# Block 0's first ff product by 26 products, the side work of five stages in another order, and the last quarter of shift and scale loaded by halves

## The chip, the cores and the metric

The kernel runs on one core of one Trainium2 chip. The time is the device time of one execution in microseconds (us), as the median of several runs. The engines of the core take their instructions in order, each from its own queue: PE (TensorE, matrix products), DVE (VectorE), ACT (ScalarE), POOL (GpSimd) and SP (SyncE, which here only issues transfers). PE's row of records has two for each matmul of a 128x256 tile.

## The reference

Two sequences of 2048 tokens with 512 features, and one condition vector of 512 for each sequence:

```
emb = silu(t) @ ada_w + ada_b
shift_msa, scale_msa, gate_msa, shift_mlp, scale_mlp, gate_mlp = split(emb, 6)
norm  = ln(x) * (1 + scale_msa) + shift_msa
h     = gelu(norm @ ssm_w1 + ssm_b1, exact)
x     = x + gate_msa * (h @ ssm_w2 + ssm_b2)
norm2 = ln(x) * (1 + scale_mlp) + shift_mlp
hf    = gelu(norm2 @ ff_w1 + ff_b1, tanh)
x     = x + gate_mlp * (hf @ ff_w2 + ff_b2)
```

All is float32. ssm_w1 and ssm_w2 are 512x512, ff_w1 is 512x1024 and ff_w2 1024x512.

## The kernel before

**Blocks and stages.** The 4096 tokens are worked in eight blocks of 512, four to a sequence, and a block stays in SBUF from its load to its store. Each has four stages: hA (first ssm product with its gelu), oA (second ssm product and residual), hC (first ff product with its gelu), oC (second ff product and residual). The stages of different blocks are interleaved; the first ones run in the order hA_0, oA_0, hA_1, oA_1, hC_0, hA_2, oC_0, hC_1. A block's norm is named n1_i ahead of hA_i and n2_i ahead of hC_i.

**Products.** No stage multiplies its matrices plainly. `group` (L573) splits both operands in four and makes seven products in place of eight, with places named P1 to P7; their order in a stage is P1, P2, P6, P5, P7, P3, P4, or, in the first three stages, P1, P2, P5, P6, P7, P3, P4. Some operands of the seven are sums of quarters: sums of weights are made once, sums of tokens (`summed`) for each block. hC of block 0 is two such groups of four matmuls a product, so 56 matmuls. From block 1 on, hC is `Second.products` (L1280) instead: a table `HK_P` of 26 products of two matmuls each, whose operands are 28 registers of weights and 24 of tokens; a row of the table names the bank of PSUM, whether it starts afresh, the two registers, and the eight parts of the result that read the bank behind it, with their signs. The tables `HK_A` (37 sums on the weights, in place) and `HK_B` (20 sums on the tokens) say how the registers come from the operands; `sums_of_registers` (L1221) issues them, each 128x256.

A part of the result is first written by ACT from PSUM, later reads are added by DVE (L1324 and L1327), and its bias and gelu follow on ACT (L1305). The next product into the same bank waits for the reads of the last.

```
for n, (b, fresh, ra, rb, reads) in enumerate(HK_P):
    for j in range(2):
        nc.tensor.matmul(ps[b][:, j, :], fa[ra][...], fb[rb]...., start=(fresh and j == 0), ...)
```

**Side work.** All that isn't a matmul of a stage is hung as small functions on the places of the stage (`hook`), and is issued right behind the product of that place, to whichever engine it uses. No scheduler moves anything: the order of the code is the order on each engine, so an instruction that waits holds up all behind it on its engine. For a norm the side work is: statistics (`mixed_stats` puts three of the four pieces on ACT, as sums and squares, and one on DVE), `root` (`ve` on DVE, a power `r` on POOL, L682 and L683) and `rest` (a Newton step on DVE), `normal` (ACT), `turn` (a transpose in 32x32 squares on DVE, L757), `move` (16 transfers of 64 KB that place the squares, on SP's and ACT's queues, L766), `moved` (shift and scale, L794), and the token sums. Further side work: the rows of the adaLN product (`rows_of`, 16 or 32 narrow matmuls on PE, L287), their transposition and bias (`modulation`), gates, the folding of gates into second weights, the residual's seeds, and loads.

**Head.** Shift and scale of the ssm branch come from the first 1024 columns of ada_w, loaded by rows of the matrix in three transfers of 1 MB, 0.5 MB and 0.5 MB (`load_ada_01`) on SP's queue, ahead of w1 in two halves. `rows_01` multiplies, `modulation_01` turns the result and adds the bias, and the tokens of block 0, transposed by PE (L773), are modulated by quarters of the features and halves of the tokens on ACT (L794) and DVE (L796). P1 of hA_0 reads features 0 to 255, P2 features 256 to 511.

**Around the change.** Weight sums of fw1: block 0's seven products need four sums of 128x1024 on POOL (`fw1_sums`, in oA_0 to oA_1). The 37 sums of `HK_A` for the later blocks follow on DVE from hC_0's second group to the end of oC_0, behind a reload of a quarter of fw1 that the earlier sums have overwritten. fw2's folds run on DVE in oA_1 and hC_0, its sums on POOL.

Of the kernel before, what the change touches and what calls it, by code (L numbers as in the profile page):

```python
# [45 lines left out]
    (1, '-', 1, 0),  # L46
    (3, '+', 3, 1),
    (11, 'n', 10, 11),
    (27, '+', 11, 1),
    (26, '-', 27, 8),  # L50
    (25, '+', 13, 15),
    (25, '-', 25, 12),
    (24, '-', 27, 2),
    (23, '-', 3, 24),
    (8, '+', 8, 23),
    (8, '+', 0, 8),
    (22, '-', 12, 26),
    (21, 'n', 1, 22),
    (22, '+', 2, 22),
    (9, '-', 9, 11),  # L60
    (20, '-', 6, 27),
    (10, '+', 6, 10),
    (19, '-', 9, 10),
    (19, 'n', 26, 19),
    (0, '-', 4, 0),
    (23, '-', 23, 0),
    (4, '+', 4, 27),
    (27, '-', 6, 19),
    (2, '-', 27, 2),
# [39 lines left out]
    (5, True, 26, 20, ((5, -1), (7, 1))),  # L109
# [3 lines left out]
    (5, False, 8, 21, ((1, 1),)),  # L113
# [6 lines left out]
    (5, False, 23, 12, ((3, 1),)),  # L120
    (0, False, 24, 16, ((0, 1),)),
    (1, True, 11, 8, ((0, -1), (2, -1))),
    (5, False, 4, 10, ((2, 1),)),
    (0, False, 2, 23, ((4, -1), (5, -1))),
    (3, False, 27, 1, ((3, 1),)),
    (5, False, 0, 9, ((0, 1),)),
# [9 lines left out]

HK_BANK = {5: "y", 2: "x", 4: "v", 0: "x", 1: "y", 3: "v"}
# [3 lines left out]
def kernel(  # L141
# [22 lines left out]
    C = 4  # L164
# [133 lines left out]
    def rows_01(pa, ks):  # L298

        for k in ks:  # L300
            w = ada_01[k // 2][:, k % 2].rearrange("p (g n m q) -> p g m n q", g=2, n=KD, q=G)
            for g in range(2):
                for m in range(P // G):
                    nc.tensor.matmul(
                        pa[m * G : (m + 1) * G, g * P : (g + 1) * P],
                        silu[:, k, :],
                        w[:, g, m],
                        start=(k == 0 and g == 0),
                        stop=(k == KD - 1),
                        tile_position=(0, m * G),  # L310
                        skip_group_check=True,
                    )

    def modulation_01(pa):

        turned = pa[:, 2 * P : 4 * P]
        nc.vector.transpose(turned, pa[:, : 2 * P])
        turned = turned.rearrange("p (g n q) -> p g n q", g=2, n=KD)
        m = const.tile([P, 2, KD, B], F32, tag="mod_0", name="mod_0")
        bias = colsT[:, R_ADA : R_ADA + 2 * KD].rearrange("p (g n) -> p g n", g=2)  # L320
        nc.vector.tensor_tensor(m, turned[:, :, :, :B], bias.unsqueeze(3).to_broadcast([P, 2, KD, B]), ALU.add)
        for part in range(2):
            mods[0, part] = m[:, part]
# [253 lines left out]
    def group(name, kdim, lhs, rhs, after, hooks, parted=(), order=ORDER, places=None):  # L577
# [4 lines left out]
        for p, place in zip(order, places or order):  # L582
# [7 lines left out]
            for j in range(2):  # L590
                for k in range(kdim):
# [24 lines left out]
    class Norm:  # L616
# [17 lines left out]
        def mixed_stats(self):  # L634

            sums, var = self.sums_on_act(), self.squares_on_act(D**-0.5)
            return sums[:3] + var[:4], self.stats(self.mv)[3:]

        def sums_on_act(self):
# [3 lines left out]
            self.unread = work.tile([P, C, D], F32, tag="blocks", name=f"unread{n}")  # L643
# [109 lines left out]
        def turn(self, c):  # L753
# [6 lines left out]
            )  # L760

# [460 lines left out]
    def sums_of_registers(program, reg, engs, copied=None, beside=()):  # L1222


        def op(n, d, f, a, b):
# [4 lines left out]
            elif f == "n":  # L1230
                nc.vector.scalar_tensor_tensor(reg[d], reg[a], -1.0, reg[b], ALU.mult, ALU.subtract)
# [38 lines left out]
    class Second:  # L1270
# [9 lines left out]
        def products(self, fa, fb, hooks, act_first=False):  # L1280


            ends = {b: n for n, (b, *_) in enumerate(HK_P)}
            starts = [(n, b) for n, (b, fresh, *_) in enumerate(HK_P) if fresh]
            stops = set(ends.values())
            for n, b in starts:
                stops |= {max([m for m in range(n) if HK_P[m][0] == b], default=ends[b])}
# [678 lines left out]
```

## Time and profile before

| | us |
|---|---|
| median of 3 runs | 577.23 (577.11 to 578.51) |
| profiled execution | 577.13 |
| its span | 575.3 |
| around the span | 1.83 |
| hC_0, seven products, 56 matmuls | 24.36 |
| hC_1, 26 products, 52 matmuls | 22.45 |

In the chain of work that ended last a row is a start, a length, an engine, the tile written and the line: `68.22 1.73 PE py_hC L592 x8` is one product of hC_0, eight records of PE. In the timeline `out<-in` names the tiles; what stands in brackets at a row's end is the engine's idle time ahead of it and what ended it. The clock granted to PE was 1.00 in every stage shown.

### The profile page before, as it was taken

The numbers are of one execution on the slowest core, as the hardware profiler recorded it, in microseconds if no ns is written. First come the engines' busy times: TensorE is split into PE (matmuls) and PEld (weight loads), VectorE is DVE, ScalarE is ACT, GpSimd is POOL, SyncE is SP. The second block draws the span as 40 slices with busy tenths as digits, with TensorE's granted clock in tenths as the row PEclk, the third lists the DMA queues.
The fourth block names the chain that finished last, engine by engine and source line by source line (L and its number), as shares of the span: only waits on it lengthen the run. The fifth ranks groups of instructions, "written<-read, shape, count | busy, mean of one in ns | idle before, by whom it ended". The sixth has DMA issues, their size and how long they took to land.

```text
span 575.3 us, 10190 instructions
## 1 busy us (share of the span) xinstructions
PE 570.6 (99%) x3467; PEld 514.5 (89%) x3467; DVE 451.9 (79%) x984; ACT 296.5 (52%) x585; POOL 439.2 (76%) x460
## 2 busy tenths in 40 slices
PE   9999999999999999999999999999999999999997
PEld 4888888888899889998899988998889999899897
DVE  4968898897789376977869877996768598897676
ACT  3727457706834875448734588325655431732430
POOL 1665449999997869889898999998994885378361
PEclk9999999999999999999999999999999999999999
DMA  8977433304205503283042921243240240031002
GB/s 329 388 232 250 101 71 92 96 38 146 63 13 148 219 2 70 96 260 126 1 93 56 338 100 24 52 108 122 101 110 1 110 131 18 1 75 74 1 1 73
DMA packets 26863, 62.30 MB, mean 108 GB/s; under 512 B 5136, under 2 KB 6204, under 8 KB 25148
## 3 DMA queue, kind: packets, MB, share of 16 engines
q1 hardware_dynamic: 22784, 55.87, 30.1%
q10 hardware_dynamic: 4028, 5.79, 3.9%
q8 instruction: 27, 0.44, 0.3%
q14 instruction: 24, 0.20, 0.1%
HBM read 35.94 MB, written 9.97 MB: 80 GB/s over the span
## 4 chain that ended last, share of the span: by engine, by line
PE 97%; DMA 2%; SPq 0%; DVE 0%; issue 0%; DVEq 0%
PE px_hC L1310 11%; PE py_hA L592 10%; PE py_hC L1310 8%; PE pv_hC L1310 8%; PE pl_oC_A_y L1160 5%; PE pv_hA L592 5%; PE py_oA L952 5%; PE pl_oC_P_y L1065 4%; PE pl_oC_B_y L1160 4%; PE py_oA L592 4%; PE py_oC L1017 4%; PE pl_oC_A_v L1160 2%; PE py_hC L592 2%; PE py_oC L592 2%; PE px_hA L592 2%; PE pl_oC_P_v L1065 2%
## 5 line engine op out<-in xcount | busy, mean ns | idle before, releaser
L683 POOL TENSOR_TENSOR r<-ve,minus_half 128x4 f32<-128x4 f32 x16 | 16.5, 1031 | 51.0 <-DVE ve L682 44.0
L794 ACT ACTIVATE nT<-nT,mod,mod 128x512 f32<-128x512 f32 x32 | 23.4, 804 | 45.3 <-DMA nT<-blocks 23.5
L1233 POOL TENSOR_TENSOR forms<-forms 128x256 f32<-128x256 f32 x56 | 42.0, 749 | 3.5
L1310 PE MATMUL py_hC<-forms,fw 128*128 128x256 f32 x168 | 40.9, 379 | 0.0
L746 ACT ACTIVATE nT<-x,nmr,rstd 128x512 f32<-128x512 f32 x36 | 26.8, 804 | 22.8 <-DVE nmr L731 20.2
L1327 DVE TENSOR_TENSOR hClo<-hClo,py_hC 128x512 f32<-128x512 f32 x42 | 28.5, 682 | 10.8 <-ACT hClo L1324 7.4
L1310 PEld LDWEIGHTS py_hC<-forms,fw 128*128 128x128 f32 x168 | 31.7, 190 | 4.6 <-DVE hClo L1327 0.2
L386 POOL TENSOR_TENSOR hSC<-hClo,hChi 128x512 f32<-128x512 f32 (+1 forms) x16 | 19.0, 1192 | 17.8 <-ACT hChi L1305 16.9
L629 DVE BATCH_NORM_STATS2 st<-x 128x6 f32<-128x512 f32 x42 | 28.4, 675 | 5.0 <-DMA x<-in_x_dram 4.9
L1327 DVE TENSOR_TENSOR hChi<-hChi,pv_hC 128x512 f32<-128x512 f32 x35 | 23.2, 679 | 9.1 <-PE pv_hC L1310 5.2
L1305 ACT ACTIVATE hClo<-hClo,colsT 128x256 f32<-128x256 f32 x56 | 25.3, 498 | 5.0 <-DVE hClo L1327 4.8
L1310 PE MATMUL px_hC<-forms,fw 128*128 128x256 f32 x112 | 27.6, 379 | 0.0
L386 POOL TENSOR_TENSOR hClo<-hClo 128x512 f32<-128x512 f32 (+1 forms) x23 | 27.0, 1179 | 0.0
L1305 ACT ACTIVATE hChi<-hChi,colsT 128x256 f32<-128x256 f32 x56 | 25.1, 496 | 1.9 <-DVE hChi L1327 1.9
L757 DVE STREAM_TRANSPOSE blocks<-nT 128x512 f32<-128x512 f32 x36 | 24.0, 691 | 1.3 <-ACT nT L746 1.3
L1324 ACT ACTIVATE hChi<-py_hC 128x512 f32<-128x512 f32 x14 | 7.6, 595 | 33.6 <-PE py_hC L1310 25.0
L1310 PEld LDWEIGHTS px_hC<-forms,fw 128*128 128x128 f32 x112 | 21.3, 190 | 2.9
L794 ACT ACTIVATE x<-x,mod 128x512 f32<-128x512 f32 x24 | 17.5, 802 | 11.8 <-DMA x<-blocks 11.8
L592 PE MATMUL py_hA<-x,w 128*128 128x256 f32 x96 | 22.7, 379 | 0.0
L1324 ACT ACTIVATE hClo<-px_hC 128x512 f32<-128x512 f32 x21 | 12.5, 596 | 19.5 <-PE px_hC L1310 15.6
L1327 DVE TENSOR_TENSOR hChi<-hChi,px_hC 128x512 f32<-128x512 f32 x28 | 19.1, 682 | 4.3 <-ACT hClo L1324 2.1
L1310 PE MATMUL px_hC<-forms,fw_s 128*128 128x256 f32 x84 | 20.5, 380 | 0.0
(555 smaller groups left out, 1930.6 us busy)
## 6 DMA issues: line engine op xcount, KB each, us to landing
x<-in_x_dram SPq DMA_DIRECT2D x13, 1024.0 KB
out_dram<-x SPq DMA_DIRECT2D x14, 512.0 KB
x<-blocks SPq DMA_DIRECT2D x96, 64.0 KB
nT<-blocks SPq DMA_DIRECT2D x88, 64.0 KB
ada<-in_L_cond_ada_w_dram SPq DMA_DIRECT2D x5, 1024.0 KB
fw<-in_L_cond_ff_w_dram SPq DMA_DIRECT2D x2, 2048.0 KB
nT<-blocks ACTq DMA_DIRECT2D x56, 64.0 KB
w<-in_L_cond_ssm_w_dram SPq DMA_DIRECT2D x2, 1024.0 KB
```

What stands on the lines that cost most here:

```text
L386: eng.tensor_tensor(out[:, r], a[:, r], b[:, r], f)
L592: nc.tensor.matmul(ps[b][j * apart][:, j, :], lhs(p, j, k), rhs(p, j, k), start=(fresh and j * (not apart) == 0 and k == 0), stop=(p in (" ...
L629: nc.vector.bn_stats(st, xs[self.i][:, c, :])
L746: nc.scalar.activation(t, x_c, AF.Identity, bias=self.nmr[:, c : c + 1], scale=self.rstd[:, c : c + 1])
L794: nc.scalar.activation(dst, src, AF.Identity, bias=shift, scale=scale)
L952: nc.tensor.matmul(ps[BANK[p]][:, j, :], hops(p, j, k), wops[p][:, k, :], start=False, stop=(k == KD // 2 - 1), skip_group_check=True,)
L1065: nc.tensor.matmul(t[:, n, :], hops.leaves[p][f][:, k, :], leaf_wops[p][f][:, k, :], start=room not in started, stop=(f in ("P2", "P3", "P ...
L1160: nc.tensor.matmul(rooms[g, b][:, at[p], :], hops.leaves[p][f][:, k, :], leaf_wops[p][f][:, k, :], start=(g, b) not in started, stop=(f in ...
L1233: eng.tensor_tensor(reg[d], reg[a], reg[b], ALU.add if f == "+" else ALU.subtract)
L1305: nc.scalar.activation(h, h, AF.Gelu_apprx_tanh, bias=fb1T[:, m : m + 1])
L1310: nc.tensor.matmul(ps[b][:, j, :], fa[ra][:, j * P : (j + 1) * P], fb[rb].rearrange("p a (c q) -> p c a q", q=Q), start=(fresh and j == 0) ...
L1327: nc.vector.tensor_tensor(dest(d), dest(d), ps[b], op)
```

## The change

1. hC_0 is `Second.products` with `HK_P0`, the 26 products of `HK_P` in another order. So the 37 weight sums and 20 token sums are made ahead of hC_0 and within it. A table `BY` says on which engine each runs: five weight sums and two token sums on DVE, 32 and 18 on POOL. The four 128x1024 sums, block 0's old token sums and the reload of a quarter of fw1 are gone. The signs in `HK_A`, `HK_B` and `HK_P` are turned so that no sum is a negated one; the numbers of the rows stay.
2. The side work from hA_0 to hA_2 is given by a table `PLAN`: for each stage and place the names of operations. In hC_0 a place is the number of a product. `BY` gives the engine of an operation, A for ACT, V for DVE, G for POOL. Folds and sums of fw2, sums of hC and the last parts of n2_1 move from oA_1 and hC_0 into hC_0's end, hA_2 and oC_0. The rows of groups 3 and 4 (`rows.0`, `rows.1`) both stand in P6 of oA_0.
3. The last quarter of shift and scale is loaded in two halves of its columns, each ahead of a half of w1. `modulation_01` works by halves of the features; the second half's rows run on PE behind the first matmul of hA_0 (`rest_of_tokens`), and its modulation follows on DVE and ACT.

The order on ACT in hA_0 and behind it, before (L646 sums and L658 squares of block 1's statistics, L869 the gelu with its table, L746 normal):

```order
L646 ACTIVATE unread_1_251,mv_1_250<-x_101 128x512 x3
L668 ACTIVATE less_1_252<-mv_1_250 128x3
L658 ACTIVATE unread_1_251,mv_1_250<-x_101,less_1_252 128x512 x3
L869 ACT_TABLE_LOAD
L869 ACTIVATE forms<-forms 128x2x256
L746 ACTIVATE nT_1_320<-x_101,nmr_1_312,rstd_1_311 128x512 x2
L876 ACTIVATE forms<-forms 128x2x256
```

and after (L776, L787, L1006 and L875 are the same four):

```order
L776 ACTIVATE unread_1_262,mv_1_261<-x_102 128x512 x3
L797 ACTIVATE less_1_263<-mv_1_261 128x3
L1006 ACT_TABLE_LOAD
L1006 ACTIVATE forms<-forms 128x2x256
L787 ACTIVATE unread_1_262,mv_1_261<-x_102,less_1_263 128x512 x3
L875 ACTIVATE nT_1_326<-x_102,nmr_1_318,rstd_1_317 128x512
L1013 ACTIVATE forms<-forms 128x2x256
L875 ACTIVATE nT_1_326<-x_102,nmr_1_318,rstd_1_317 128x512
```

Table load and first gelu now stand ahead of the squares, and the second gelu ahead of the second of the four pieces of `normal`.

The order on DVE in hA_1, before (L868 is P2's read of `px_hA`, L858 the reads of `py_hA` and `pv_hA`, L386 token sums of n1_1, L682 `ve` of n2_0):

```order
L858 TENSOR_TENSOR hA_492<-py_hA_0_493,colsT 128x2x256
L386 TENSOR_TENSOR nT_1_320<-nT_1_320 128x4x2x64
L868 TENSOR_TENSOR hA_492<-px_hA_0_500,hA_492 128x2x256
L386 TENSOR_TENSOR nS_1_368<-nT_1_320,nS_1_368 128x512
L629 BN_STATS st_0_3_508<-x_90 128x6
L630 BN_AGGR mv_0_369<-st_0_3_508 128x2
L682 TENSOR_SCALAR ve_0_511<-mv_0_369 128x4
L858 TENSOR_TENSOR hA_492<-pv_hA_0_515,colsT 128x2x256
L858 TENSOR_TENSOR hA_492<-py_hA_0_493,colsT 128x2x256
```

and after (L1005, L995, L500, L811):

```order
L747 BN_STATS st_0_3_500<-x_90 128x6
L748 BN_AGGR mv_0_487<-st_0_3_500 128x2
L443 STREAM_TRANSPOSE pada_427<-pada_427 128x128
L447 TENSOR_TENSOR mod_1_506<-pada_427,colsT 128x8
L995 TENSOR_TENSOR hA_517<-py_hA_0_518,colsT 128x2x256
L500 TENSOR_TENSOR nS_1_485<-nT_1_326,nS_1_485 128x512
L811 TENSOR_SCALAR ve_0_527<-mv_0_487 128x4
L1005 TENSOR_TENSOR hA_517<-px_hA_0_532,hA_517 128x2x256
L500 TENSOR_TENSOR nT_1_326<-nT_1_326 128x4x2x64
L995 TENSOR_TENSOR hA_517<-py_hA_0_518,colsT 128x2x256
```

`ve_0`, with the statistics ahead of it, stands in front of P2's read of `px_hA`; the read of `pv_hA` has gone to ACT.

The order on POOL between the power of n2_0 and that of block 2, and up to hC_0's tokens, before:

```order
L683 TENSOR_TENSOR r_0_512<-ve_0_511,minus_half 128x4
L386 TENSOR_TENSOR fw_s<-fw_s,fw_118 128x1024
L386 TENSOR_TENSOR fw_118<-fw_118 128x2x512
L386 TENSOR_TENSOR fw_s<-fw_118,fw_s 128x1024
L386 TENSOR_TENSOR nS_0_617<-nT_0_538 128x512
L682 TENSOR_SCALAR ve_2_663<-mv_2_616 128x4
L683 TENSOR_TENSOR r_2_664<-ve_2_663,minus_half 128x4
```

and after, from behind the first twelve weight sums that follow the power of n2_0 (L1368 is `sums_of_registers`; its rows of `fw` are weight sums, of `forms` and `nT` token sums; L500 are token sums of hA_1):

```order
L500 TENSOR_TENSOR hSA_645<-hA_517,hSA_645 128x512
L500 TENSOR_TENSOR hA_517<-hA_517 128x2x256
L1368 TENSOR_TENSOR fw_s<-fw_119 128x256
L1368 TENSOR_TENSOR fw_119<-fw_s,fw_119 128x256
L812 TENSOR_TENSOR r_2_690<-ve_2_689,minus_half 128x4
L1368 TENSOR_TENSOR fw_119<-fw_119 128x256
L1368 TENSOR_TENSOR forms<-nT_0_573 128x256
L1368 TENSOR_TENSOR forms<-forms,nT_0_573 128x256
L1368 TENSOR_TENSOR forms<-forms 128x256
L1368 TENSOR_TENSOR forms<-nT_0_573,forms 128x256 x2
```

The four sums of 128x1024 are replaced by sums of 128x256, the sums of hA_1 are partly on POOL, and behind the second power follow one weight sum and the token sums.

```diff
-    (11, 'n', 10, 11),
+    (11, '+', 10, 11),
...
+HK_P0 = [HK_P[n] for n in (1, 0, 6, 2, 9, 4, 5, 3, 8, 11, 7, 12, 13, 14, 10, 15, 19, 16, 18, 17, 20, 21, 22, 23, 24, 25)]
...
+PLAN = {
...
+    "hA_1": {
...
+        "P1": "n2_0.stats.3 n1_1.sum.3 n2_0.stats.7 n2_0.root.0 a.10",
...
+    "a": "VGVVGGGVGGGGGGGGGGGGGGGGGVGGGGGGGGGGG",
+    "b": "VVGGGGGGGGGGGGGGGGGG",
+}
+BESIDE, COPIED, ON_SCALAR, ON_ACT = (), (3, 1), (8, 8, 3), (('P5',), ('P6', 'P5'))
...
+    def load_last_ada_01(h):
+        k, cols = KD - 1, slice(h * D // 2, (h + 1) * D // 2)
+        nc.sync.dma_start(
+            out=ada_01[k // 2][:, k % 2].rearrange("p (g n) -> p g n", g=2)[:, :, cols],
+            in_=ada_w[k * P : (k + 1) * P, : 2 * D].rearrange("p (g n) -> p g n", g=2)[:, :, cols],
+        )
+
     load_ada_01((0, 1))
     load_ada_01((2,))
-    load_ada_01((3,))
+    load_last_ada_01(0)
     w1_sb = const.tile([P, KD, D], F32, tag="w1", name="w1")
     load_half("w1", w1, w1_sb, 0)
+    load_last_ada_01(1)
     load_half("w1", w1, w1_sb, 1)
...
+    def modulation_01(pa, h):
+
+        turned = pa[:, (2 + h) * P : (3 + h) * P]
+        nc.vector.transpose(turned, pa[:, h * P : (h + 1) * P])
+        turned = turned.rearrange("p (g n q) -> p g n q", g=2, n=KD // 2)
+        n = slice(h * KD // 2, (h + 1) * KD // 2)
...
+        def move_some(self, eng, pieces):
+
+            for a, m in pieces:
+                eng.dma_start(
+                    out=self.nT[m * Q : (m + 1) * Q, a, :],
+                    in_=self.bl[a * Q : (a + 1) * Q, m].rearrange("p k c q -> p (k c q)"),
+                )
...
-        def products(self, fa, fb, hooks, act_first=False):
+        def products(self, fa, fb, hooks, act_first=False, products=HK_P):
...
-    rows_01(pada_01, (3,))
+    rows_01(pada_01, (3,), (0,))
     for c in (0, 3, 2):
         n1[0].transpose(c, pts, c == 3)
-    modulation_01(pada_01)
-    for h in range(2):
-        for k in range(KD):
-            n1[0].modulate(k, pts, nc.vector if k % 2 else None, h)
+
+    def modulated(part):
+        modulation_01(pada_01, part)
+        for h in range(2):
+            for k in (2 * part, 2 * part + 1):
+                n1[0].modulate(k, pts, nc.vector if k % 2 else None, h)
+
+    modulated(0)
+
+    def rest_of_tokens():
+        rows_01(pada_01, (3,), (1,))
+        modulated(1)
...
-    hC.group(0, n2[0].ops, hooks, ("P6", "P5"))
...
-    def fw1_quarter():
-
-        half = slice(KH // 2 * P, KH * P)
-        nc.scalar.dma_start(
-            out=fw1_sb[:, : KD // 2, half], in_=fw1[: D // 2, half].rearrange("(k p) n -> p k n", p=P)
-        )
...
-    hC.group(1, n2[0].ops, hooks)
...
+    hooks = begin("hA_0")
+    hooks["P1", 0, 0] = [rest_of_tokens]
+    hA[0] = First(0, n1[0].ops, hooks, FIRST, hA_0)
+    w2_ops = found["w2"][0]
+    residual("oA_0", 0, hA[0], w2_ops, KD // 2, begin("oA_0"), order=FIRST)
+    hooks = begin("hA_1")
+    hA[1] = First(1, n1[1].ops, hooks, FIRST, on_act=ON_ACT[0])
+    residual("oA_1", 1, hA[1], w2_ops, KD // 2, begin("oA_1"))
+    hooks = begin("hC_0")
+    hC.products(fa, fb[0], hooks, True, HK_P0)
```

More of the change, by code (lines that the diff above doesn't have):

```diff
@@ new lines @@
+    at("b", *[lambda n=n: form_0(n) for n in range(len(HK_B))])
+    at("table", lambda: nc.scalar.activation(unread, minus_half, AF.Gelu_apprx_tanh))
+    room = forms[:, 8:].rearrange("p (c n) a r -> p c (n a r)", c=C)
+    later("n1_2.stats", 6, lambda: sum(n1[2].mixed_stats(1, room), []))
+    at("n1_2.root", n1[2].root)
+    at("n1_2.rest", n1[2].rest)
+    turned("n1_2", n1[2], ON_SCALAR[2], ENGS["n1_2.normal"])
+    at("n1_2.modulated", *n1[2].moved(ENGS["n1_2.modulated"]))
+    later("n1_2.sum", 4, lambda: n1[2].summed(ENGS["n1_2.sum"]))
```

446 lines of the change are left out of this document (260 added, 186 removed).

## The prediction

> **What bounds the kernel now.** I read the page's busy shares and the shares of the chain that ended last, then the busy time of each stage, then the chain itself.
>
> ```profile
> span 575.3 us, 10190 instructions
> PE 570.6 (99%) x3467; PEld 514.5 (89%) x3467; DVE 451.9 (79%) x984; ACT 296.5 (52%) x585; POOL 439.2 (76%) x460
> PE 97%; DMA 2%; SPq 0%; DVE 0%; issue 0%; DVEq 0%
> ```
>
> TensorE (PE) is busy 99% of the span and makes 97% of the chain. A matmul removed is time saved, and a wait added to PE costs its whole length; the work of the other engines counts only where PE waits for it.
>
> ```profile
> 68.22:92.58 24.36, 24.36 (x113) 21.19 (x113) 21.92 (x39) 15.82 (x25) 15.70 (x26) 1.00 0.29 72
> 92.58:104.67 12.09, 12.09 (x58) 10.64 (x57) 11.57 (x16) 7.38 (x14) 12.09 (x14) 1.00 0.41 98
> 104.67:128.84 24.17, 24.17 (x113) 21.28 (x113) 21.66 (x30) 9.38 (x24) 23.78 (x29) 1.00 0.18 66
> 128.84:151.29 22.45, 22.45 (x106) 19.61 (x105) 17.75 (x36) 15.63 (x30) 21.98 (x24) 1.00 0.30 102
> ```
>
> A row gives a window, its length, then the busy time of PE, weight loads, DVE, ACT and POOL, the granted clock, the DMA share and the rate. The windows are hC_0 (block 0's first ff product), hA_2, oC_0, and hC_1, which has the form that the change gives to hC_0. PE fills all four. POOL has 8.7 us left in hC_0, none in hA_2.
>
> **The change part by part.** First the matmuls.
>
> ```profile
> 68.22 1.73 PE py_hC L592 x8
> 75.12 1.92 PE py_hC L592 x8
> 145.25 1.73 PE pv_hC L1310 x8
> ```
>
> hC_0 is 14 products of 4 matmuls, 1.73 us each (8 records, two for a matmul), 0.432 a matmul; the row at 75.12 is 0.19 longer. hC_1 is 26 products of 2 matmuls, 0.863 each (145.25 holds two), 52 matmuls instead of 56, free of waits. Term 1: 22.45 - 24.36 = **-1.91**, if block 0 runs the 26 as block 1 does.
>
> In oA_0 the row matmuls of groups 3 and 4 stand in two places, and the product behind each is longer:
>
> ```profile
> 31.02 1.92 PE px_oA L592 x8
> 37.41 1.93 PE py_oA L592 x8
> ```
>
> Side by side they leave one such product. Term 2: **-0.20**.
>
> The head. The last quarter of shift and scale comes in two halves of 0.26 MB, half of w1 between them.
>
> ```profile
> 11.70:14.50 2.80, 2.76 (x31) 2.29 (x32) 1.92 (x5) 1.54 (x4) 0.00 (x0) 1.00 1.08 421
> 11.74 0.64 PE L304 MATMUL pada<-ada,w_t 128*32 128x128 f32 x16
> 12.31 1.53 PE L773 MATMUL pt<-w_t,blocks 128*128 128x128 f32 x12
> 13.22 1.90 DVE L796 TENSOR_SCALAR nT<-pt,mod 128x256 f32<-128x256 f32 x4
> 13.82 1.99 PE L592 MATMUL py_hA<-nT,w 128*128 128x256 f32 x8
> 14.50 1.26 POOL L386 TENSOR_TENSOR w_s<-w 128x512 f32<-128x512 f32 x1 [4.90 <-DMA w<-in_L_cond_ssm_w_dram]
> 15.04 1.28 DVE L386 TENSOR_TENSOR nS<-nT 128x512 f32<-128x512 f32 x1
> 15.65 1.89 PE L592 MATMUL px_hA<-nT,w 128*128 128x256 f32 x8
> ```
>
> Before, the quarter has landed by 11.70 and w1 by 14.50, at 421 GB/s. After, the first half is there 0.26 MB / 421 GB/s = 0.62 earlier, at 11.08; half the row matmuls (0.32) and the 12 transposes (1.53) put the first matmul of hA_0 near 13.1 instead of 13.82. The second half lands 0.52 MB before 14.50, at 13.25; its row matmuls run behind the first matmul of P1. DVE turns them only after the sum that now stands ahead (1.28, from about 13.4 to 14.7), then transposes and adds bias (0.5) and modulates a quarter (1.90 / 4 = 0.48): P2 has operands at about 15.8, against 15.65. With the start-up of PE behind the wait I put P7 of hA_0 0.25 late. Term 3: **+0.25**, between -0.7 (the earlier start is kept) and +0.7 (P2 needs the next pair of modulates as well).
>
> ACT in hA_0: table load and gelu now stand ahead of the three squares of block 1's statistics.
>
> ```profile
> 20.63 0.71 ACT L658 ACTIVATE unread<-x,less 128x512 f32<-128x512 f32 x1
> 21.44 1.28 ACT L869 ACT_TABLE_LOAD   x1
> 22.65 0.17 DVE L682 TENSOR_SCALAR ve<-mv 128x4 f32<-128x4 f32 x1
> 32.48 1.29 DVE L757 STREAM_TRANSPOSE blocks<-nT 128x512 f32<-128x512 f32 x2
> 41.04 1.52 ACT L794 ACTIVATE nT<-nT,mod 128x512 f32<-128x512 f32 x2 [10.44 <-DMA fw_t<-in_L_cond_ada_b_dram]
> ```
>
> The squares end near 23.25 instead of 21.4, `ve` at 23.35 instead of 22.65, and the turns of n1_1 (last one 33.77 before) and its modulation (41.04) come 0.7 later. The first piece, 0.76 long, is then there at 42.5, and hA_1 starts at 42.78 + 0.05 by terms 2 and 3: hidden with 0.3 to spare. Its price is zero, at most +0.4 if the piece is as late again; should the head gain instead, the gain ends here.
>
> hA_1: `ve` of n2_0 now stands on DVE ahead of the read of `px_hA` for P2.
>
> ```profile
> 46.27 0.69 DVE L868 TENSOR_TENSOR hA<-px_hA,hA 128x512 f32<-128x512 f32 x1
> 48.49 0.17 DVE L682 TENSOR_SCALAR ve<-mv 128x4 f32<-128x4 f32 x1
> 50.70 1.93 PE py_hA L592 x8
> ```
>
> It waits for ACT's last square. Queued behind it are the read of `px_hA`, a sum, and the read that frees `py_hA` for P7. With one more modulated piece ahead on ACT the squares end at about 48.8; three DVE operations at 0.69 then end near 50.95 and P7 starts near 51.0 instead of 50.70. Term 4: **+0.30**, between 0 (squares on time) and +0.9 (another 0.6 on ACT).
>
> hC_0. All 37 weight sums (32 on POOL) and 20 token sums (18 on POOL) must now be made by then. Removed are four weight sums of 2.36 and four token sums of 1.27, 14.5 us of POOL.
>
> ```profile
> 36.74 2.36 POOL L386 TENSOR_TENSOR fw_s<-fw 128x1024 f32<-128x1024 f32 x1
> 48.74 1.02 POOL L683 TENSOR_TENSOR r<-ve,minus_half 128x4 f32<-128x4 f32 x1 [9.64 <-DVE ve L682]
> 57.62 4.17 ACTq L766 DMA_DIRECT2D nT<-blocks  x6
> 63.34 2.93 ACT L794 ACTIVATE nT<-nT,mod,mod 128x512 f32<-128x512 f32 x4 [5.97 <-DMA gates<-w_t]
> 65.07 0.18 DVE L630 BATCH_NORM_AGGREGATE mv<-st 128x2 f32<-128x6 f32 x1
> 64.93 1.27 POOL L386 TENSOR_TENSOR nS<-nT 128x512 f32<-128x512 f32 x1 [8.18 <-ACT nT L794]
> 128.97 2.33 POOL L1233 TENSOR_TENSOR forms<-forms 128x256 f32<-128x256 f32 x3
> L386 POOL TENSOR_TENSOR hClo<-hClo 128x256 f32<-128x256 f32 x7 | 6.6, 956 | 0.0
> ```
>
> A 128x256 sum costs POOL 0.78 in a row of three (2.33 / 3, in hC_1), 0.956 in the dearest group of the trace. I take 0.78, since DVE in the new hC_0 reads PSUM as it does in hC_1. POOL takes the power for n2_0 at about 49.1 to 50.1, then 12 weight sums, two sums of 1.27 and two weight sums: 14 x 0.78 + 2.5 = 13.4, done at 63.5. The next power waits for `ve_2`, which I put at 64.3: block 2's statistics ended at 65.25 on DVE alone (65.07 + 0.18), and ACT now takes a quarter of them. So 0.8 is to spare. The tokens: the turns end about 1.8 later than before, at 57.2, behind term 4 and work that now stands ahead of them; the last issue is at 62.9 instead of 61.79 (57.62 + 4.17), the landing 1.55 behind it as before (63.34 - 61.79), at 64.45; three pieces on ACT of 0.73 (2.93 / 4) are ready at 66.7, one on DVE earlier. From 66.75 POOL makes 16 token sums: the ninth at 73.8, the sixteenth at 79.2. hC_0 starts at 68.22 - 0.20 + 0.25 + 0.30 = 68.57, so product 6 needs the ninth at 73.75 and product 12 the sixteenth at 78.9 without waits. I add 0.15 at product 6 and 0.6 at product 8, whose bank DVE has still to read (0.68 a read, and two reads stand in the queue against 0.863 a product). Term 5: **+0.75**, between 0 (as in hC_1) and +2.0 (a whole read late at three places).
>
> Hidden: fw2's folds and sums and the sums of hC move into hA_2 and oC_0, where DVE loses its weight sums; their last operand (P6 of oC_0) I find at 110.1 against 110.9 needed. The reload of a quarter of fw1 goes, a transfer that PE never waited for. The token moves of n2_0 pass SP and ACT as before, eight pieces on each.
>
> Sum: -1.91 - 0.20 + 0.25 + 0.30 + 0.75 = -0.81; 577.13 (the profiled execution: span 575.3 and 1.83 around it, 0.10 under the median of 577.23) - 0.81 = **576.3 us**.
>
> [...]
>
> ```profile
> 126.27 0.41 DVE L1233 TENSOR_TENSOR fw<-fw,fw_s 128x256 f32<-128x256 f32 x1
> L1233 DVE TENSOR_TENSOR fw<-fw 128x256 f32<-128x256 f32 x11 | 9.8, 889 | 0.0
> L1233 POOL TENSOR_TENSOR forms<-forms 128x256 f32<-128x256 f32 x56 | 42.0, 749 | 3.5
> ```
>
> [...] By the rows the 32 sums take POOL 24 us, about what goes (14.5) and what stood idle in hC_0 (8.7).
>
> **The rivals.** (a) No new waits: the 26 products run as in hC_1, the head and `ve` cost nothing. -1.91 - 0.20 = -2.1, **575.0**. For it: hC_1 has no wait with the same work around it. Against it: hC_1's tokens were ready long before, here the sums chase the products.
>
> (b) POOL is late, the case on the other side. At 0.956 a sum the 14 weight sums end at 50.1 + 13.4 + 2.5 = 66.0 instead of 63.5, power and one sum at 68.0, sixteen token sums at 83.3, against 79.7 needed with term 5's waits: 3.6 of waiting instead of 0.75, **579.1**. It decides from about 0.89 a sum, where the waiting of 1.56 eats the gain. For it: POOL sums cost 0.956 where DVE adds from SBUF. Against it: DVE has few such sums between 50 and 80 us.
>
> [...]
>
> (c) The work moved behind hC_0 fills POOL from 84 to 110 us (26 us, and hA_2 left it nothing before); if its sums are 6% dearer, 1.6, the operand of oC_0's P6 comes 0.8 late: **577.1**. Against it: DVE is relieved of 26 sums there.
>
> **How the numbers follow.** The forecast has 0.42, (a) 0.29, (b) 0.22, (c) 0.07. The forecast's own range is 575.5 to 577.6 (term 5 at 0 and at 2). The range reaches from 574.7, (a) with half of the head's gain kept, to 579.4, (b) a little dearer. What differs by under 0.3% (1.73 us) can't be told from no change: faster is below 575.5, slower above 578.96. Faster takes most of (a) and the lower end of the forecast, 0.26 + 0.08 = 0.34; slower most of (b) and a mishap of the others, 0.17 + 0.05 = 0.22; the same 0.44.
>
> **What would show it.** Right: 52 matmuls in hC_0, 22.5 to 23.5 us from its first to hA_2's first; the first matmul of hA_0 at 13.1 and P2 near 15.8; one row of 1.92 in oA_0; P7 of hA_1 near 51.0; POOL's sums at 0.75 to 0.80 and PE waiting for them at product 6. Wrong: sums above 0.89, PE waiting for tokens at the start of hC_0, a wait in hA_1's P1, or a product of oC_0 behind a POOL sum. Most of all a token move that lands later than 1.55 us behind its issue would put the whole token chain, and hC_0, late.

## The result and the profile after

The changed kernel takes 576.52 us (median, 576.03 to 576.71) where the kernel before takes 577.15 (median of the runs on the same chips); the ratio is 0.9986 (0.9979 to 0.9992). The forecast was 576.3; by the 0.3% that the prediction set for it, this counts as the same time. First the page of the changed kernel, and its stages hC_0, hA_2 and oC_0 as windows (window, length, busy time of PE, weight loads, DVE, ACT and POOL, clock, DMA share, rate):

```profile
span 574.7 us, 10197 instructions
PE 569.9 (99%) x3459; PEld 512.3 (89%) x3459; DVE 436.2 (76%) x971; ACT 301.7 (52%) x601; POOL 456.9 (79%) x479
```

```profile
68.85:91.96 23.11, 23.11 (x105) 19.35 (x105) 21.52 (x38) 15.59 (x29) 19.32 (x32) 1.00 0.26 64
91.96:104.04 12.08, 12.08 (x57) 10.63 (x57) 10.24 (x17) 9.14 (x18) 11.92 (x10) 1.00 0.08 18
104.04:128.21 24.17, 24.17 (x114) 21.28 (x113) 4.15 (x6) 9.95 (x24) 23.54 (x25) 1.00 0.33 101
```

The span is 0.6 us shorter, PE is still busy 99% of it, and 16 us of DVE's work are gone and 18 of POOL's have come. hC_0 takes 23.11 instead of 24.36, a gain of 1.25; hA_2 and oC_0 are as long as before. The rest is in the chain of the changed kernel, with the starts of oA_0 (timeline) and of hA_1 (chain) in the kernel before ahead of it:

```profile
28.12 1.89 PE L592 MATMUL py_oA<-w,forms 128*128 128x256 f32 x8
42.78 1.73 PE py_hA L592 x8
```

```profile
43.03 1.99 PE py_hA L708 x8
60.04 1.90 PE py_oA L708 x8
69.71 1.83 PE py_hC L1441 x8
74.14 2.89 PE px_hC L1441 x12
77.89 1.79 PE px_hC L1441 x8
83.14 1.91 PE pv_hC L1441 x8
```

hA_1 starts at 43.03 (42.78 before) and its first product is 0.26 long over 1.73; P6 of oA_1 (60.04) is 0.17 long; hC_0 starts at 68.85 (68.22 before), and its 26 products, 22.45 without waits, have four places that are longer, 0.65 together. Stage by stage, after against before: the head +0.51 (first matmul of oA_0, below), oA_0's rows -0.34, the start of hA_1 +0.34, oA_1 +0.12, hC_0 -1.25; together -0.62, and from hA_2 on the two kernels run in step.

### The profile page after: what moved, and what is told of

Read it like the earlier page. It is cut to its first block, busy times and chain, and to the rows that moved or that the text cites. A ratio compares the mean times of both kernels' runs of the same rounds, so it can differ in the third digit from the quotient of the medians.

```text
span 574.7 us, 10197 instructions
## 1 busy us (share of the span) xinstructions
PE 569.9 (99%) x3459; PEld 512.3 (89%) x3459; DVE 436.2 (76%) x971; ACT 301.7 (52%) x601; POOL 456.9 (79%) x479
## 4 chain that ended last, share of the span: by engine, by line
PE 92%; DVE 2%; SPq 1%; ACT 0%; issue 0%; POOL 0%; DMA 0%; ACTq 0%; DVEq 0%
PE px_hC L1441 12%; PE py_hC L1441 10%; PE pv_hC L1441 10%; PE py_hA L708 8%; PE pl_oC_A_y L1297 5%; PE py_oA L1089 5%; PE pv_hA L708 4%; PE pl_oC_P_y L1202 4%; PE pl_oC_B_y L1297 4%; PE py_oC L1154 4%; PE pl_oC_A_v L1297 2%; PE py_oA L708 2%; PE py_oC L708 2%; PE pl_oC_P_v L1202 2%; PE pl_oA_y L1104 2%; PE px_hA L708 2%
## 5 line engine op out<-in xcount | busy, mean ns | idle before, releaser
L1368 POOL TENSOR_TENSOR forms<-forms 128x256 f32<-128x256 f32 x64 | 47.1, 735 | 3.8
L1441 PE MATMUL py_hC<-forms,fw 128*128 128x256 f32 x192 | 46.7, 379 | 0.0
L1441 PEld LDWEIGHTS py_hC<-forms,fw 128*128 128x128 f32 x192 | 36.3, 190 | 5.2 <-DVE hClo L1458 0.2
L875 ACT ACTIVATE nT<-x,nmr,rstd 128x512 f32<-128x512 f32 x33 | 24.9, 804 | 18.8 <-DVE nmr L860 16.6
L500 POOL TENSOR_TENSOR hSC<-hClo,hChi 128x512 f32<-128x512 f32 x14 | 18.1, 1289 | 18.4 <-ACT hChi L1436 16.2
L1441 PE MATMUL px_hC<-forms,fw 128*128 128x256 f32 x128 | 31.5, 379 | 0.0
L1436 ACT ACTIVATE hClo<-hClo,colsT 128x256 f32<-128x256 f32 x64 | 28.8, 498 | 5.0 <-DVE hClo L1458 4.8
L1436 ACT ACTIVATE hChi<-hChi,colsT 128x256 f32<-128x256 f32 x64 | 28.7, 496 | 2.9 <-DVE hChi L1458 2.9
L500 POOL TENSOR_TENSOR hClo<-hClo 128x512 f32<-128x512 f32 (+1 forms) x21 | 26.1, 1242 | 0.1
L931 ACT ACTIVATE x<-x,mod 128x512 f32<-128x512 f32 x24 | 17.6, 802 | 13.1 <-DMA x<-blocks 13.1
L1441 PE MATMUL px_hC<-forms,fw_s 128*128 128x256 f32 x96 | 23.6, 382 | 0.0
L1441 PE MATMUL pv_hC<-nT,fw 128*128 128x256 f32 x96 | 23.3, 379 | 0.0
L1455 ACT ACTIVATE hClo<-px_hC 128x512 f32<-128x512 f32 x22 | 13.1, 596 | 19.5 <-PE px_hC L1441 15.6
L1458 DVE TENSOR_TENSOR hClo<-hClo,px_hC 128x512 f32<-128x512 f32 x26 | 17.6, 677 | 7.5 <-PE px_hC L1441 7.0
```

The lines of the kernel that those rows point to most:

```text
L500: eng.tensor_tensor(out[:, r], a[:, r], b[:, r], f)
L875: nc.scalar.activation(t, x_c, AF.Identity, bias=self.nmr[:, c : c + 1], scale=self.rstd[:, c : c + 1])
L931: nc.scalar.activation(dst, src, AF.Identity, bias=shift, scale=scale)
L1368: eng.tensor_tensor(reg[d], reg[a], reg[b], ALU.add if f == "+" else ALU.subtract)
L1436: nc.scalar.activation(h, h, AF.Gelu_apprx_tanh, bias=fb1T[:, m : m + 1])
L1441: nc.tensor.matmul(ps[b][:, j, :], fa[ra][:, j * P : (j + 1) * P], fb[rb].rearrange("p a (c q) -> p c a q", q=Q), start=(fresh and j == 0) ...
```

## The experiments

Each run has its own median beside that of the kernel before, measured on the same chip (577.10 to 577.23); a stage is told from the profiled execution. Medians that lie within 0.3 of one another have overlapping runs, and there the trace is what tells them apart. A trace shows one execution of each kernel.

**1. The head: the quarter in one load.** Part 3 of the change is undone in the changed kernel, and done alone in the kernel before.

```diff
-    load_last_ada_01(0)
+    load_ada_01((3,))
...
-    load_last_ada_01(1)
...
-    rows_01(pada_01, (3,), (0,))
+    rows_01(pada_01, (3,))
...
-    hooks["P1", 0, 0] = [rest_of_tokens]
```

> The changed kernel with part 3 undone: the last quarter of shift and scale in one load ahead of w1, all tokens of block 0 modulated before the first matmul. Theory A (the 0.5 us that the head lost is given back by the rows of oA_0, and PE then waits for block 1's tokens at the start of hA_1, whatever the head does): oA_0 starts 0.5 earlier, near 28.1 on the line of PE, but hA_1 starts only as much earlier as block 1's statistics do, 0.3, since x of block 1 lands 0.3 earlier; 576.2. Theory B (the head's loss runs through to the end): hA_1 starts 0.5 earlier, 576.0. Theory C (the halves help after all): slower than 576.5.

> The kernel before with part 3 alone: the quarter in halves, rows of the second half behind the first matmul of hA_0, modulation by halves. Theory A (the halves lose 0.5 in the head, nothing in the old order takes it back, PE having no wait at hA_1's start there): 577.6. The prediction's term 3: 577.4. Theory B (the loss is swallowed further on, or the halves gain): 577.1 or less.

Undone: 576.32 (576.03 to 576.92), ratio 0.9982 (0.9973 to 0.9990). Done alone: 577.78 (577.47 to 579.67), ratio 1.0011 (1.0001 to 1.0020), so 0.6 slower. The timeline of PE and DVE in the head of the changed kernel:

```profile
13.37 0.70 PE L708 MATMUL py_hA<-nT,w 128*128 128x256 f32 x2
13.57 0.54 DVE L933 TENSOR_SCALAR nT<-pt,mod 128x256 f32<-128x256 f32 x1 [0.26 <-PE pt L910]
14.22 0.69 DVE L500 TENSOR_TENSOR nS<-nT 128x512 f32<-128x512 f32 x1
14.83 0.32 DVE L431 STREAM_TRANSPOSE pada<-pada 128x128 f32<-128x128 f32 x1
15.39 1.00 DVE L933 TENSOR_SCALAR nT<-pt,mod 128x256 f32<-128x256 f32 x2
16.00 1.99 PE L708 MATMUL px_hA<-nT,w 128*128 128x256 f32 x8
28.63 1.89 PE L708 MATMUL py_oA<-w,forms 128*128 128x256 f32 x8
```

The first matmul starts 0.45 earlier than before (13.82), but the tokens of P2 hang on DVE's second transpose and modulation behind a sum, and P2 starts 0.35 later (15.65 before), oA_0 0.51 later (28.12). In the kernel before with part 3 alone oA_0 starts at 28.63 too, and nothing takes it back. Undone in the changed kernel, oA_0 starts at 28.25, but hA_1 at 43.11, no earlier than with the halves:

```profile
28.25 1.89 PE L707 MATMUL py_oA<-w,forms 128*128 128x256 f32 x8
34.27 6.24 SPq L893 DMA_DIRECT2D nT<-blocks  x8
43.11 1.99 PE L707 MATMUL py_hA<-nT,w 128*128 128x256 f32 x8 [0.53 <-ACT nT L930]
```

So the loss of the head is real (theory A for the run alone), and in the changed kernel it is covered by hA_1's wait for block 1's tokens. That the tokens did not come 0.3 earlier here is due to the token moves: the turns ended 0.34 earlier, but the last move was issued at 40.51, by SP after 6.24, where in the changed kernel it was at 40.44, by ACT after 5.83 (SP took 5.48 there). In ten traces ACT's modulation of these tokens begins 1.65 to 1.81 behind the end of the last issue on either queue (2.13 in the run with part 3 alone), so it is the moves that it waits for, hardly the `DMA fw_t` that its row names. Why an issue takes longer in one run than in another no run here tells.

**2. The squares ahead of the table load.** Their old place on ACT, in the changed kernel and together with the whole quarter.

```diff
-        "P1": "... n1_0.sum.3 n1_1.stats.3",
-        "P2": "n1_0.sum.2 n1_1.stats.4",
-        "P5": "n1_1.stats.7 n1_1.stats.6",
-        "P6": "n1_1.stats.5 n1_1.root.0 ...",
+        "P1": "... n1_0.sum.3 n1_1.stats.3 n1_1.stats.4 n1_1.stats.5 n1_1.stats.6",
+        "P2": "n1_0.sum.2",
+        "P5": "n1_1.stats.7",
+        "P6": "n1_1.root.0 ...",
```

> The changed kernel with the three squares of block 1's statistics ahead of the table load and the first gelu, as before the change. Theory A (the late squares make block 1's tokens late, and the start of hA_1 with them): ve at 22.9 instead of 23.56, turns and tokens 0.7 earlier, no wait at hA_1's start and no slow first product behind it, 0.5 less: 576.0. Theory B (the token moves and their transfers set it, not the squares): tokens near 42.0 still, under 0.2 less, 576.4. Theory C (the gelu 2 us later holds up hA_0's sums and oA_0): a new wait of PE in oA_0, 576.5 or more.

> Both edits of the two runs before: whole quarter, and squares ahead of the table load. Theory A: each removes its own half of what the early stages lost, 0.5 in the head and 0.5 at hA_1's start, 575.5, and hC_0 starts near 67.9. Theory B (hC_0's tokens, not PE, set when hC_0 can go on): hC_0 starts 1.0 earlier but waits longer inside, its 23.1 becoming 23.5 to 24, 576.0 to 576.5.

575.91 (575.62 to 576.34), ratio 0.9973 (0.9963 to 0.9983), and with both edits 575.74 (575.50 to 575.86), ratio 0.9971 (0.9959 to 0.9983). ACT, DVE and ACT's token moves in the changed kernel, then, of the run with the squares first, the moves, ACT and the chain:

```profile
22.73 0.71 ACT L787 ACTIVATE unread<-x,less 128x512 f32<-128x512 f32 x1
23.56 0.17 DVE L811 TENSOR_SCALAR ve<-mv 128x4 f32<-128x4 f32 x1 [1.38 <-ACT unread L787]
34.61 5.83 ACTq L894 DMA_DIRECT2D nT<-blocks  x8
42.16 2.23 ACT L931 ACTIVATE nT<-nT,mod 128x512 f32<-128x512 f32 x3 [10.63 <-DMA fw_t<-in_L_cond_ada_b_dram]
```

```profile
34.23 5.17 ACTq L894 DMA_DIRECT2D nT<-blocks  x8
41.35 2.23 ACT L931 ACTIVATE nT<-nT,mod 128x512 f32<-128x512 f32 x3 [10.32 <-DMA fw_t<-in_L_cond_ada_b_dram]
42.88 1.73 PE py_hA L708 x8
68.27 0.86 PE pv_hC L1441 x4
91.06 1.73 PE py_hA L708 x8
```

In the changed kernel DVE waits 1.38 for the last square, and ACT modulates block 1's tokens from 42.16. With the squares first it does so from 41.35: 0.38 of the 0.81 come from the turns, the rest nearly all from moves that are issued faster (ACT 5.17 instead of 5.83, so that SP's, 5.48 in both, are now the last). hA_1 then starts without a wait, its first product is 1.73 again, and hC_0 starts 0.58 earlier. The later gelu costs nothing. That is theory A, with a share of B. With both edits hC_0 starts at 67.80, 0.47 earlier still, but hA_2 only 0.1 earlier (90.96): its 22.79 become 23.16, theory B of that run. hC_0 is then held by the work that makes its operands (4, below): n2_0's tokens are there at 64.00, only 0.08 earlier than with the squares alone.

**3. The rows of groups 3 and 4 apart**, in the run with the squares first, where no wait hides it.

```diff
-        "P1": "... loads.0 loads.1",
-        "P2": "n1_1.move.1 loads.2",
+        "P1": "... loads.0 loads.1 rows.0",
+        "P2": "mods.0 n1_1.move.1 loads.2",
```

> Beside the run with the squares ahead (575.91, no wait at hA_1's start): the same with the rows of groups 3 and 4 apart again, in P1 and P6 of oA_0, as before the change. The prediction's term 2: one more slow product, 0.20 more, 576.1. Theory A (the two stages of the trace differ by 0.49, since each of the two places costs PE a restart on the way into the narrow matmuls and one on the way out): hA_1 starts 0.5 later and the whole comes to 576.4, unless the tokens of hC_0 swallow a part of it.

575.96 (575.85 to 576.11), ratio 0.9972 (0.9961 to 0.9983), against 575.91: not told apart by the median. In the chains hA_1 starts at 43.15 instead of 42.88. oA_0 is 14.50 long as before the change, 14.16 with the rows side by side: they save 0.34. The 0.27 reach the start of hA_2 (91.32 against 91.06).

**4. What hC_0 waits for.** Where weight loads stood still in hC_0 of the changed kernel, the time in brackets, with what ended it:

```profile
69.55 0.73 PEld L1441 LDWEIGHTS py_hC<-forms,fw_s 128*128 128x128 f32 x4 [0.24 <-POOL forms L1368]
73.93 0.73 PEld L1441 LDWEIGHTS px_hC<-nT,fw_s 128*128 128x128 f32 x4 [0.20 <-POOL nT L1368]
75.89 0.73 PEld L1441 LDWEIGHTS px_hC<-forms,fw_s 128*128 128x128 f32 x4 [0.37 <-DVE hChi L1458]
77.69 1.59 PEld L1441 LDWEIGHTS px_hC<-forms,fw_s 128*128 128x128 f32 x8 [0.20 <-DVE hChi L1458]
83.92 0.73 PEld L1441 LDWEIGHTS pv_hC<-nT,fw_s 128*128 128x128 f32 x4 [0.32 <-POOL nT L1368]
```

Products 1, 6 and 17 seem to wait for POOL, products 8 and 10 for DVE's reads of their banks. In the next run the 18 token sums on POOL are left out, so that block 0's products take zeros from an early fill; this time is not that of the whole computation.

```diff
+            if program is HK_B and eng is nc.gpsimd and len(engs) > 1:
+                if n == 2:
+                    nc.gpsimd.memset(forms[:, 8:14], 0.0)
+                return
```

> The changed kernel without block 0's 18 token sums on POOL (left out: their registers hold zeros from one early fill, so block 0's result is not the reference's). Theory A (of hC_0's 0.66 of waiting, POOL's sums make 0.4 and DVE's reads 0.25): hC_0 22.7 long instead of 23.11, 576.1. Theory B (DVE's reads make all of it): 23.1, no change. Term 5 said 0.75, of it 0.15 for the sums.

576.13 (575.93 to 576.88), ratio 0.9980 (0.9971 to 0.9989). hC_0 is 22.82 long, 0.29 shorter; the waits at products 8 and 10 are as they were (0.44 and 0.20), those of products 1 and 17 are gone, and at product 6 a gap of 0.14 is left. Theory A, with 0.3 for the sums and 0.37 for the reads. Product 6 also hangs on ACT's read of product 3, which stands behind a piece of block 2's norm.

So the order of the sums should count. On top of both edits of 2:

```diff
-            "a.31 copies.0 b.2 b.4 table.0 b.0 b.1 b.3"
-            " n1_2.rest.0 b.5 b.6 b.7"
+            "a.31 copies.0 b.2 table.0 b.0 b.1 b.3 b.4"
+            " n1_2.rest.0 b.5 b.6 b.7 b.11"
...
-        10: "b.19 n2_1.stats.2",
+        10: "b.14 n2_1.stats.2",
```

> Beside the run with both edits (575.74, hC_0 23.16 long): the same with three of block 0's token sums taken earlier on POOL (the one for product 1 ahead of the one for product 2, the one for product 6 three places earlier, the one for product 17 ahead of a weight-free one for the end). Theory A (0.4 of hC_0's waits are single token sums in the wrong order, the other 0.25 DVE's reads of a bank that is used again two products later): hC_0 22.75 long, 575.3. Theory B (the start of the whole row of sums is what is late, the order changes nothing): 575.7.

575.59 (575.06 to 575.90), ratio 0.9967 (0.9954 to 0.9980), the lowest median of all. hC_0 is 22.88 long instead of 23.16, the waits of products 1 and 17 are gone. What is left stands at products 6 to 8, in the chain of this run 2.96 for three products of 0.863:

```profile
67.92 0.86 PE pv_hC L1440 x4
73.10 2.96 PE px_hC L1440 x12
90.80 1.73 PE py_hA L707 x8
```

One step further, for ACT's read of product 3:

```diff
-    "n2_0.modulated": "VAAA",
+    "n2_0.modulated": "VVAA",
...
-        2: "n1_2.normal.2 n1_2.turn.0 a.27 n1_2.turn.1",
-        3: "a.33 n1_2.turn.2",
-        4: "a.32",
+        2: "n1_2.turn.0 a.27 n1_2.turn.1",
+        3: "n1_2.normal.2 a.31 a.33",
+        4: "a.32 n1_2.turn.2",
```

> Beside the run with the sums in order (575.59, hC_0 22.88 long): the same with one more quarter of n2_0 modulated on DVE instead of ACT, one weight sum and one piece of block 2's norm behind the reads of product 3. Theory A (what is left in hC_0 is ACT's read of product 3, queued behind the norm, and DVE's read of product 6, inherent in the order of the products): the first goes, hC_0 22.65 long, 575.35. Theory B (DVE is late instead by the work it takes over): 575.6 or more.

575.75 (575.49 to 576.63), ratio 0.9974 (0.9964 to 0.9985). hC_0 is 22.76 long, 0.12 shorter, but the profiled execution had lost 0.8 on the way there (a row matmul waited for its load in hA_0, a statistic of block 2 for x), so the two runs can't be ranked.

**5. How much room POOL has.** Sums that nobody reads, ahead of hC_0's first token sum on POOL, four and then two.

```diff
+    spare = forms[:, 7].rearrange("p a r -> p (a r)")
+    at("pad", *[lambda: nc.gpsimd.tensor_tensor(spare, fa[0], fa[1], ALU.add)] * 4)
...
-            "a.31 copies.0 b.2 b.4 table.0 b.0 b.1 b.3"
+            "a.31 pad.0 pad.1 pad.2 pad.3 copies.0 b.2 b.4 table.0 b.0 b.1 b.3"
```

> The changed kernel with four more weight sums on POOL, written where nobody reads, right ahead of hC_0's first token sum: 4 x 0.72 = 2.9 of POOL. In the changed kernel POOL stood idle 0.9 there. Theory A (rival (b) of the prediction: the token sums chase the products and POOL has under 1 us left): 2.0 more of waiting in hC_0, 578.5. Theory B (POOL has room, the waits in hC_0 are those of DVE's reads): under 0.5 more, 577.0.

> The changed kernel with two more sums on POOL ahead of hC_0's tokens instead of four: 1.5 of POOL, 0.6 more than it stood idle. With four, PE waited 2.12 in one place, and in the 3.5 us behind it the granted clock was 0.73 and 0.50. Theory A (a wait of PE costs its length; the clock falls only behind a long one): one wait of 0.8, clock 1.00 behind it, 577.1. Theory B (the clock falls behind this wait too): 578 or more.

Four: 579.72 (578.31 to 580.22), ratio 1.0034 (1.0020 to 1.0047). Two: 577.22 (576.91 to 577.59), ratio 0.9997 (0.9988 to 1.0006). POOL at that place in the changed kernel, then PE and two windows of the run with four, then the run with two:

```profile
67.27 0.73 POOL L1368 TENSOR_TENSOR forms<-nT 128x256 f32<-128x256 f32 x1 [0.90 <-ACT nT L931]
```

```profile
71.61 1.13 PE L1441 MATMUL py_hC<-forms,fw_s 128*128 128x256 f32 x4 [2.12 <-POOL forms L1368]
72.58 1.70 PE L1441 MATMUL py_hC<-forms,fw 128*128 128x256 f32 x4
71.60:74.20 2.60, 2.59 (x9) 2.19 (x10) 1.35 (x3) 0.11 (x1) 2.52 (x4) 0.73 0.00 0
74.20:76.00 1.80, 1.80 (x6) 1.44 (x5) 1.45 (x3) 1.30 (x2) 1.72 (x4) 0.50 0.00 0
```

```profile
70.54 0.73 PEld L1441 LDWEIGHTS py_hC<-forms,fw_s 128*128 128x128 f32 x4 [1.06 <-POOL forms L1368]
70.50:73.00 2.50, 2.46 (x11) 2.20 (x12) 1.35 (x4) 2.11 (x5) 2.42 (x4) 1.00 0.00 2
```

POOL stands idle 0.90 ahead of the first token sum, waiting for the tokens, and what goes beyond that PE pays: +0.7 with two sums, theory A of both runs. The prediction's rival (b) was a true mechanism; it did not come in because a sum took 0.73 here and not 0.956. With four sums PE paid more than its wait: behind 2.12 of waiting the granted clock was 0.73 and 0.50 in the two windows shown, a record of one product took 1.70 where 1.03 is usual, and about 2.0 went on top of the wait. The two clocks are means of their windows; ahead of them, from 69.50 to 71.60, the clock was 1.00, from 76.00 to 78.00 it was 0.95, and from 78.00 to 82.00 it was 1.00 again. With two sums PE itself stood 0.66 (its weight loads 1.06), and the clock stayed at 1.00. The quickest executions with four sums, 578.31 and 578.43, are near the 578.5 of theory A; the mean clock was 1.0 in them (and in one of 579.55), 0.997 in the profiled execution of 580.09.

**6. `ve` of n2_0 behind P2's read**, in the changed kernel.

```diff
-        "P1": "n2_0.stats.3 n1_1.sum.3 n2_0.stats.7 n2_0.root.0 a.10",
-        "P2": "a.16 ...",
+        "P1": "n2_0.stats.3 n1_1.sum.3 n2_0.stats.7 a.10",
+        "P2": "n2_0.root.0 a.16 ...",
```

> The changed kernel with ve and power of n2_0 back behind P2's read of px_hA in hA_1. The prediction's term 4: P7 of hA_1 starts 0.3 earlier, 0.3 less in all, 576.2. Theory A (in the changed kernel's trace the read that frees P7's bank ends 50.96 and P7 starts 51.14, so ve in front cost P7 nothing; behind the read the power comes 0.2 to 0.7 later, the tokens of n2_0 as well): no gain at P7, hC_0's waits 0.2 to 0.7 longer, 576.6 to 577.1.

576.16 (575.98 to 576.83), ratio 0.9977 (0.9968 to 0.9986), 0.36 under the changed kernel. The edit also lets a weight sum, `a.10`, go ahead of n2_0's power on POOL. Of the changed kernel first a later weight sum, the one piece of n2_0's `normal` that DVE makes, and the weight load of P6 of oA_1; then, of this run, `ve`, ACT's `normal`, the same weight sum, the same piece on DVE, and the modulation of n2_0's tokens:

```profile
54.47 0.74 POOL L1368 TENSOR_TENSOR fw_s<-fw,fw_s 128x256 f32<-128x256 f32 x1
54.48 1.01 DVE L879 TENSOR_SCALAR nT<-x,rstd,nmr 128x512 f32<-128x512 f32 x1
59.95 1.59 PEld L708 LDWEIGHTS py_oA<-w_s,hSA 128*128 128x128 f32 x8 [0.31 <-DVE hSA L500]
```

```profile
48.96 0.17 DVE L811 TENSOR_SCALAR ve<-mv 128x4 f32<-128x4 f32 x1 [0.53 <-ACT unread L787]
51.95 1.52 ACT L875 ACTIVATE nT<-x,nmr,rstd 128x512 f32<-128x512 f32 x2 [1.27 <-DVE nmr L860]
54.12 0.72 POOL L1368 TENSOR_TENSOR fw_s<-fw,fw_s 128x256 f32<-128x256 f32 x1
54.45 0.69 DVE L879 TENSOR_SCALAR nT<-x,rstd,nmr 128x512 f32<-128x512 f32 x1
64.58 1.52 ACT L931 ACTIVATE nT<-nT,mod,mod 128x512 f32<-128x512 f32 x2 [0.75 <-DMA nT<-blocks]
```

P7 starts 8.18 behind hA_1's start as in the changed kernel, so it never waited. Nor was theory A right that the power costs time here: `ve` waits for ACT's last square at 48.96 (48.98 in the changed kernel), and DVE now reads `px_hA` in that time. The power ends 0.35 later, but the Newton step on it stands behind a read on DVE that ends at 50.90 (50.96 in the changed kernel). The gelu behind the read comes 0.96 earlier, but this is lost again: ACT then waits 1.27 for DVE (0.33 in the changed kernel), and its `normal` starts at 51.95 instead of 52.00.

What the rows show in its place is on POOL, which makes the extra weight sum while it waits for `ve`, so that its later sums come some 0.35 earlier. In the changed kernel DVE's piece starts together with a POOL sum and takes 1.01; here the sum starts 0.33 ahead of it, and the piece takes 0.69. Behind it on DVE stand the turns of n2_0 and the token sums of hA_1: P6 of oA_1 doesn't wait, n2_0's tokens are there at 64.58 instead of 64.97, and hC_0 takes 22.91. Both theories named the wrong place. No run moves the weight sum alone, so its share is read from the rows, not shown by an edit.

The same piece took 0.60 in the run with the squares first and 0.97 with both edits. So a part of the gain in 2, and of what both edits lost again in hC_0, depends on how this piece and a POOL sum happen to meet.

**7. Two token sums on DVE**, on top of the run with the sums in order.

```diff
-    "b": "VVGGGGGGGGGGGGGGGGGG",
+    "b": "VVVVGGGGGGGGGGGGGGGG",
```

> Beside the run with the sums in order (575.59): the same with two more of block 0's token sums, the first ones, on DVE instead of POOL. On DVE such a sum took 0.42 there, on POOL 0.73. [...] Theory B (DVE is then late with the residual and the reads of hC_0): 575.9 or more.

577.51 (577.11 to 577.86), ratio 1.0000 (0.9991 to 1.0009): 1.9 slower than without; hC_0 is 24.49 long instead of 22.88. DVE, POOL and PE in this run:

```profile
67.77 0.83 DVE L1367 TENSOR_TENSOR forms<-nT,forms 128x256 f32<-128x256 f32 x1
67.48 0.84 POOL L1367 TENSOR_TENSOR forms<-forms,nT 128x256 f32<-128x256 f32 x1 [1.34 <-DVE forms L1367]
71.00 0.68 DVE L1049 TENSOR_TENSOR x<-py_oA,x 128x512 f32<-128x512 f32 x1
71.83 1.10 PE L1440 MATMUL py_hC<-forms,fw 128*128 128x256 f32 x4 [1.18 <-DVE x L1049]
```

Here a sum on DVE beside one on POOL takes 0.83 and POOL's takes 0.84; in the run with the sums in order they took 0.42 and 0.73. The sums end no earlier than on POOL, and behind them on DVE stands the residual's last read of oA_1, whose bank product 2 needs: PE waits 1.18. Moving them costs at least the 1.6 us of hC_0 here.

## Why the prediction was right

The time came out 0.2 us above the forecast, inside the likeliest case and its own range. The main step, hC_0 by 26 products with token sums that chase them, is as forecast; two of the smaller steps are not. The terms, one by one:

- Term 1, the 26 products: right. Without token sums and with 0.37 of reads hC_0 is 22.82, so 22.45 stands.
- Term 2, the rows side by side: right in kind, too small; 0.34 for 0.20.
- Term 3, the head: right in sign and mechanism, too small; +0.51 for +0.25. The first matmul came at 13.37 and not at 13.1: PE was still at the transposes of 11.06, so the first half's row matmuls ran at 11.64 and not at 11.08. P2 started at 16.00, not 15.8, since DVE's second modulation waited for PE's transposes (13.57), which the term left out. Run 1 shows the loss by itself.
- The squares, priced at nothing: wrong. The tokens were there at 42.16 + 0.82 and not at 42.5, and hA_1 paid 0.07 of waiting and 0.26 of a slow first product (the +0.34 above). The step took 0.7 for the shift of `ve`; it was 0.91, and ACT's token moves took 0.7 longer to issue (5.83 instead of 5.14), which the step had taken as unchanged: the last issue ended 1.21 later. Run 2 shows it.
- Term 4, `ve` in hA_1: wrong. +0.30 was forecast at P7, and P7 lost nothing: the read that frees its bank ended at 50.96, as forecast, but PE had the row matmuls ahead of P7 until 51.14. That run 6 gained 0.36 is luck for this term, since it came another way. What the changed kernel paid is 0.12 at P6 of oA_1, behind DVE's piece of the norm beside a POOL sum, which no term had; a part of term 5 is its doing.
- Term 5, hC_0's waits: +0.66 for +0.75. Its split was off: the sums made about 0.3, twice what the term gave them, the reads 0.37 in place of 0.6. A token sum took 0.73 to 0.79, close to the 0.78 that was taken.

The misses on the loss side (+0.26, +0.34, +0.12) and on the gain side (-0.14, -0.30, -0.09) nearly cancel, so the total is better than its parts, and that it is only 0.2 off is in part luck. Of the rivals, (a) fell by 1.5 us of waits and slow places. (b) is 0.90 us of POOL away, as run 5 shows; its price was also summed wrongly, since 83.3 against the 78.9 needed without waits is 4.4 of waiting and 579.9, with the turn at 0.87 a sum and not at 0.89. (c) did not come in: oC_0 is 24.17 long, as before.

## What to carry to other kernels

Where PE is never idle, a stage's saving is worth what is left after the next place at which PE waits for an operand: undoing the head's loss brought hA_1 no earlier while it waited for tokens, and with that wait gone 0.37 of its 0.47 were lost again in hC_0. Before moving work between engines, list what stands behind it on the new engine: two sums in front of one read of a bank cost 1.6 in hC_0. In a row of short sums, their order against the order of the products that need them is worth a gain of its own (0.28 in hC_0). An edit that shifts one engine by 0.3 also changes which operations of two engines meet, so read the rows behind it before its gain is put down to the thing that was moved.

## What the runs showed of the hardware that was not expected

A wait of PE of 2.12 us was followed by a fall of the granted clock (run with four more sums): 0.73 in the mean of 71.60 to 74.20, which begins at the wait's end, 0.50 from 74.20 to 76.00, 0.95 from 76.00 to 78.00, and 1.00 from there to 82.00. In the chain the four products behind the wait took 2.67, 1.71 and 1.03 where 1.73, 0.86 and 0.86 are usual, 1.96 more, so that the wait cost about 4.1. A wait of 0.66 (two more sums) and one of 1.18 (two sums on DVE) left the clock at 1.00 (to 75.00 in both). In the chain of the changed kernel the rows behind shorter waits are 0.10 (69.71), 0.17 (60.04) and 0.26 (43.03) longer than 1.73, which a sum over waits has to carry.

DVE's piece of n2_0's norm, 128x512 from SBUF, took 1.00 to 1.01 in six traces in which it started together with a POOL sum, and 0.60 and 0.69 in the two where the sum was 0.42 and 0.33 ahead. In all eight it ended 0.28 to 0.30 behind the sum.

The issue of eight token moves of 64 KB took SP 5.48 in one run and 6.24 in another with the same order of issues (1, above), a difference larger than most of the terms above.
